# A new layout for the head of a four-layer graph kernel: loads in order of need, weights prepared in six stages

## The chip, the cores and the metric

The kernel runs on one core of a Trainium2 chip. The metric is device time in microseconds (us), the median over several executions; all runs told here were of the same fast state, and the granted TensorE clock over a whole run was 0.98 to 0.99 of full speed in all of them. Only differences of runs that shared a chip are compared as ratios. Times inside a run are counted from the start of its span.

## The reference

```python
h = maximum(layernorm(x), 0); x = x + gated_graph(h)      # layer 0: three sigmoid gates per node,
                                                          #   messages over adj, its transpose, itself
h = maximum(layernorm(x), 0); x = x + attention(h)        # layer 1: causal, adj added to the scores
h = maximum(layernorm(x), 0); x = x + three_convs(h)      # layer 2: (adj*S) @ (h @ W) with W1, W2, W3
h = maximum(layernorm(x), 0); x = x + mlp_batchnorm(h)    # layer 3: normalised adjacency, two linear
                                                          #   maps, batch norm over the whole batch
```

`x` is 128 x 128 x 256, `adj` 128 x 128, all float32. W1 is 256 x 512, W2 512 x 1024, W3 1024 x 256. The batch is worked in 32 groups of 4. Layers 0 to 2 run group by group; layer 3 needs sums over all groups.

## The kernel before

TensorE products are done with seven instead of eight block products, which needs *combinations* (sums and differences of quarters) of both operands. Those of the weights are formed once, in the head, on GpSimd:

```python
def seven_of(b, name):
    b11, b21, b12, b22 = quarters(b)
    extra = weights.tile(...)
    t1, t2, t4n = (extra[:, i] for i in range(3))
    nc.gpsimd.tensor_tensor(t1, b12, b11, ALU.subtract)
    nc.gpsimd.tensor_tensor(t2, b22, t1, ALU.subtract)
    nc.gpsimd.tensor_tensor(t4n, b21, t2, ALU.subtract)
    nc.gpsimd.tensor_tensor(b12, b22, b12, ALU.subtract)
    return b11, b21, b22, t4n, t1, t2, b12
```

The head loads weights from two queues, stages them in a pool that is closed before the "work" pool is opened, and prepares them all before layer 0 of group 0. Then the first two groups alternate:

```python
with tc.tile_pool(name="prep", bufs=1) as prep:
    def turned(dst, src, nr, name):            # transpose on TensorE, copy on VectorE
        ...
        nc.vector.tensor_copy(dst[:, c, :]..., pt)
    ...                                        # adjacency, wqkv, m_qk, w_vo, degrees
    turned(bw1T, bw1, FC, "bw1T")
    turned(bw2t, bw2, DC, "bw2T")
    nc.scalar.dma_start(BW2T, bw2t)
...
w = passA.enter_context(tc.tile_pool(name="work", bufs=2))
...
for _ in layer0(0):
    pass
QR, VR = (seven_of(m, n) for m, n in ((m_qk, "m_qk"), (w_vo, "w_vo")))
W1R = seven_of(w1, "w1")
first, second = layer1(0), layer0(1)
while next(first, first) is not first:
    if next(second, second) is second and not W2R:
        W2R += seven_of(w2, "w2"); W3R += seven_of(w3, "w3"); BW1R += seven_of(bw1T, "bw1T")
```

Layer 0 of a group: the gate products `gs`, then the *gate combinations*, twelve VectorE instructions on two operands in SBUF each (SBUF is the engines' on-chip memory), then products and the addition to x. The profile calls both `cmb` and `bias` by the name of the tile they lie in, `m`:

```python
for b in range(G):                             # G = 4, three gates each: 12 instructions
    nc.vector.scalar_tensor_tensor(gs, h[:, b, :], 1.0, gw[:, i, :], ..., accum_out=gl[...])
...
for b in range(G):
    nc.vector.scalar_tensor_tensor(cmb[:, b, :], aout, gt[:, b, 1:2], cmb[:, b, :], ...)
    nc.vector.scalar_tensor_tensor(cmb[:, b, :], ident, gt[:, b, 2:3], cmb[:, b, :], ...)
for b in range(G):
    nc.vector.scalar_tensor_tensor(bias[:, b, :], oeb, gt[:, b, 1:2], bias[:, b, :], ...)
...
nc.vector.scalar_tensor_tensor(xt, bias, 0.0, xt, ALU.max, ALU.add)     # "x add"
```

## Time and profile before

| | before |
|---|---|
| median of the first 3 runs | 2714.4 us (2713.95 to 2714.87) |
| span of the profiled run | 2709.8 us |
| TensorE busy | 95% |
| first h of group 0 | 29.89 us |
| end of the gate products (gl) | 43.31 us |
| end of the x add of group 0 | 54.86 us |
| first product of layer 2 of group 0 (pu_x) | 99.64 us |
| store of group 0 after layer 2 | 172.79 us |

The last rows are moments on one chain, read from the order of time. Names that begin with p followed by another name (pu_x, pqv, pm, ps, py) are results of TensorE. The differences between neighbours are the stages. The profile's lines for them are in the prediction.

### The profile page before, as it was taken

What the parts mean: (1) busy time and instruction counts of PE and PEld (TensorE: products, weight loads), DVE (VectorE), ACT (ScalarE), POOL (GpSimd) and SP (SyncE); (2) the same over time, 40 slices, a digit from 0 to 9 for tenths busy, and PEclk for the clock granted to TensorE, in tenths of its full rate; (3) what the DMA queues carried; (4) which work ended last, traced back from release to release, by engine and by line L of the source; (5) the groups of instructions that cost most, each with busy time, mean ns of one, the idle gap of its engine ahead of it and who ended that gap; (6) DMA issues with size and microseconds to landing.
All of it is one profiled execution on the core that took longest, in us unless ns stands there. A gap on an engine that the chain in (4) does not pass through costs nothing.

```text
span 2709.8 us, 39136 instructions
## 1 busy us (share of the span) xinstructions
PE 2582.3 (95%) x14831; PEld 2220.0 (82%) x14831; DVE 1899.8 (70%) x4624; ACT 1232.8 (45%) x2435; POOL 469.1 (17%) x484
## 2 busy tenths in 40 slices
PE   3899999999999999999999999999999999979994
PEld 2788888988988988888888898898898888944443
DVE  5677777777777777777777777777877775444445
ACT  2444444445444444544444444544444443334445
POOL 4111111111111111111111111111111111110001
PEclk6899999999999999999999999999999999989997
DMA  3000000000000000000000000000000000034449
GB/s 135 1 17 32 32 32 32 24 32 24 32 32 32 32 32 32 32 23 25 32 32 32 32 24 32 24 32 32 32 32 32 32 24 16 32 148 155 155 169 366
DMA packets 61758, 142.17 MB, mean 52 GB/s; under 512 B 4594, under 2 KB 39940, under 8 KB 57604
## 3 DMA queue, kind: packets, MB, share of 16 engines
q1 hardware_dynamic: 50224, 103.36, 10.6%
q0 software_dynamic: 9216, 33.56, 3.1%
q10 hardware_dynamic: 2132, 2.76, 0.3%
q8 instruction: 117, 1.92, 0.3%
q14 instruction: 69, 0.57, 0.1%
HBM read 73.08 MB, written 66.58 MB: 52 GB/s over the span
## 4 chain that ended last, share of the span: by engine, by line
PE 63%; DVE 21%; ACT 5%; issue 5%; POOL 4%; DMA 2%; ACTq 0%; SPq 0%; DVEq 0%; POOLq 0%
PE p_x L338 10%; PE po L729 8%; PE p_x L321 6%; PE pu_x L321 4%; PE p_z L338 4%; PE pz_x L338 4%; DVE st L258 4%; POOL rs L145 4%; ACT h L267 3%; DVE uT L280 3%; PE p_z L321 2%; PE p_y L338 2%; PE pg L277 2%; PE ps L481 2%; PE pz_z L338 2%
## 5 line engine op out<-in xcount | busy, mean ns | idle before, releaser
L267 ACT ACTIVATE h<-x,sh,rs 128x256 f32<-128x256 f32 x512 | 268.7, 591 | 138.4 <-DVE sh L264 126.2
L145 POOL TENSOR_TENSOR rs<-rs,nhalf 128x4 f32<-128x4 f32 x128 | 130.1, 1016 | 813.4 <-DVE rs L143 813.4
L338 PE MATMUL p_x<-uT,w 128*128 128x256 f32 x1024 | 242.2, 379 | 0.0
L353 ACT COPY p_t<-p_x 128x512 f32<-128x512 f32 (+1 forms) x192 | 98.3, 512 | 301.5 <-PE p_x L338 288.4
L568 ACT ACTIVATE h2T<-h2T 128x512 f32<-128x512 f32 x192 | 120.4, 627 | 233.8 <-DVE h2T L567 233.8
L390 DVE SCALAR_TENSOR_TENSOR gs<-h,gw 128x256 f32<-128x256 f32 x384 | 203.7, 530 | 19.4 <-ACT h L267 6.8
L729 PE MATMUL po<-zi,bw2T 128*128 128x512 f32 x496 | 213.0, 592 | 0.0
L338 PEld LDWEIGHTS p_x<-uT,w 128*128 128x128 f32 x1024 | 189.7, 190 | 23.1
L258 DVE BATCH_NORM_STATS2 st<-x 128x6 f32<-128x256 f32 x512 | 190.7, 414 | 2.9 <-DMA x<-in_x_dram 1.8
L729 PEld LDWEIGHTS po<-zi,bw2T 128*128 128x128 f32 x496 | 94.2, 190 | 118.6 <-issue 107.9
L722 ACT ACTIVATE zi<-zi,sh_bn,sc_bn 128x512 f32<-128x512 f32 x124 | 90.5, 802 | 116.8 <-DMA zi<-z 110.7
L598 POOL DMA_DIRECT2D x<-x x32 | 19.8, 620 | 691.5 <-DVE x L595 691.5
L733 DVE TENSOR_SCALAR o<-po,vecs 128x512 f32<-128x512 f32 x64 | 48.1, 751 | 128.6 <-PE po L729 128.6
L277 PEld LDWEIGHTS pmu<-a2T,u 128*128 128x128 f32 x1024 | 119.8, 192 | 15.0 <-issue 7.4
L321 PEld LDWEIGHTS p_x<-w,h2T 128*128 128x128 f32 x1024 | 124.3, 192 | 3.3
L338 PE MATMUL p_x<-us,w_s 128*128 128x256 f32 x512 | 126.2, 380 | 0.0
L321 PE MATMUL p_x<-w,h2T 128*128 128x128 f32 x1024 | 124.6, 275 | 0.0
L338 PE MATMUL p_x<-uT,w_s 128*128 128x256 f32 x512 | 124.3, 385 | 0.3 <-DVE h2T L567 0.3
L338 PE MATMUL p_y<-uT,w 128*128 128x256 f32 x512 | 121.1, 379 | 0.0
L338 PE MATMUL p_z<-us,w 128*128 128x256 f32 x512 | 121.0, 379 | 0.0
L338 PE MATMUL p_z<-us,w_s 128*128 128x256 f32 x512 | 121.0, 379 | 0.0
L277 PE MATMUL pmu<-a2T,u 128*128 128x128 f32 x1024 | 119.9, 275 | 0.0
(252 smaller groups left out, 6016.1 us busy)
## 6 DMA issues: line engine op xcount, KB each, us to landing
z<-zo SPq DMA_DIRECT2D x62, 512.0 KB, 2.6
zi<-z SPq DMA_DIRECT2D x31, 1024.0 KB, 4.8
x<-in_x_dram SPq DMA_DIRECT2D x32, 512.0 KB, 3.9
x<-x POOLq DMA_DIRECT2D x32, 512.0 KB, 3.0
x3i<-x POOLq DMA_DIRECT2D x32, 512.0 KB, 6.6
out_dram<-x3i SPq DMA_DIRECT2D x64, 256.0 KB, 7.0
w<-in_L_gnn_W_dram SPq DMA_DIRECT2D x1, 2048.0 KB, 11.8
bw<-in_L_gnn_W_dram ACTq DMA_DIRECT2D x2, 512.0 KB
```

Source lines behind the costliest of these rows:

```text
L145: nc.gpsimd.tensor_tensor(dst, src, nhalf[:, : dst.shape[1]], ALU.pow)
L258: nc.vector.bn_stats(st[:, b, :], xt[:, b, :])
L267: nc.scalar.activation(h[:, b, :], xt[:, b, :], AF.Relu, bias=sh[:, b : b + 1], scale=rs[:, b : b + 1])
L277: nc.tensor.matmul(pm[:, b, :], src[:, b, c * P : (c + 1) * P], aT, start=True, stop=True)
L280: nc.vector.tensor_copy(dst[:, c, :], pm.rearrange("p b n -> p (b n)"))
L321: nc.tensor.matmul(pb[:, rr, :], a_r[r][:, c, rr * P : (rr + 1) * P], b_r[r][:, c, :wide], start=(first and rr == 0 and c == 0), stop=(c = ...
L338: nc.tensor.matmul(pb[:, jj, :], b_r[r][:, c, at : at + P], a_r[r][:, c, :], start=(first and jj == 0 and c == 0), stop=(c == nk - 1), ski ...
L353: nc.scalar.copy(t, pb)
L390: nc.vector.scalar_tensor_tensor(gs, h[:, b, :], 1.0, gw[:, i, :], ALU.mult, ALU.mult, accum_out=gl[:, b, i : i + 1],)
L568: nc.scalar.activation(dst, dst, AF.Relu)
L722: nc.scalar.activation(z[j], z[j], AF.Relu, bias=sh1[:, j : j + 1], scale=sc1[:, j : j + 1],)
L729: nc.tensor.matmul(po, bw2T[:, j, i * P : (i + 1) * P], z[j], start=(j == 0), stop=(j == FC - 1),)
```

## The change

The intent is to start the first group sooner and to spread the preparation of the weights over the time in which the engines are idle anyway. Staging tiles move from their own pool into two buffers that layer 2 uses later. The large loads go to SyncE's queue in order of need, which frees ScalarE of issuing them. The copies of the turned weights go from VectorE to ScalarE. The preparation becomes a generator of six stages, and a string says in which order its stages (p), layer 0 and 1 of group 0 (a, B) and layer 0 of group 1 (A) take their steps.

```diff
+    wide1 = w.tile([P, HC2 * T], FP, tag="h2T", name="wide1", bufs=1)
+    wide2 = w.tile([P, 3 * HC2 * T // 4], FP, tag="h2s", name="wide2", bufs=1)
+    wqkv, wT = part_of(wide2, DC, 3 * D), part_of(wide2, 3 * DC, D)
     ... (cut: the other staging tiles likewise)
+    nc.sync.dma_start(wqkv, rows(Wqkv))
+    nc.sync.dma_start(wo, rows(Wo))
+    nc.sync.dma_start(eb, edge_bias)
+    nc.sync.dma_start(oeb, out_edge_bias)
+    load_x(1)
+    nc.sync.dma_start(w1, rows(W1))
+    nc.sync.dma_start(w2, rows(W2))
+    load_x(2)
+    nc.sync.dma_start(w3, rows(W3))
     ... (cut: bw1, bw2 and the vectors)
-                nc.vector.tensor_copy(dst[:, c, :]..., pt)
+            nc.scalar.copy(dst[:, c, :]..., pt)
+    def prepare():
+        turned(wT, wqkv, DC, "wqkvT")
         ... (cut: products m_qk, w_vo)
+        yield
+        SETS["q"], SETS["v"] = seven_of(m_qk, "m_qk"), seven_of(w_vo, "w_vo")
+        yield
+        nc.vector.tensor_tensor(a2T, adjT, adjT, ALU.mult)
+        SETS["1"] = seven_of(w1, "w1")
+        yield
+        SETS["2"] = seven_of(w2, "w2")
+        SETS["3"] = seven_of(w3, "w3")
+        yield
+        turned(bw1T, bw1, FC, "bw1T")
+        turned(bw2t, bw2, DC, "bw2T")
+        nc.sync.dma_start(BW2T, bw2t)
+        yield
         ... (cut: degrees, vectors)
+        yield
+        SETS["b"] = seven_of(bw1T, "bw1T")
-    (cut: the loop that alternates the first two groups)
+    FILL = "apaapaaaaBBABBBBBBBpBABBBApBABBpABBpABBABB"
+    stream = {"a": layer0(0), "p": prepare(), "B": layer1(0), "A": part(layer0, 1)}
+    for k in FILL:
+        next(stream[k])
```

More of the change, by code (lines that the diff above doesn't have):

```diff
@@ L129, with part_of @@
     nc.gpsimd.memset(nhalf, -0.5)
-    nc.scalar.dma_start(eb, edge_bias)
-    nc.scalar.dma_start(oeb, out_edge_bias)
-    for i, w in enumerate((gate_weight, out_gate_weight, loop_gate)):
+    nc.gpsimd.memset(gb, 0.0)
+    for i, v in enumerate((gate_weight, out_gate_weight, loop_gate)):
         nc.scalar.dma_start(
-            gw[:, i, :], bass.AP(tensor=w.tensor, offset=w.offset, ap=[[0, P], [1, D]])
+            gw[:, i, :], bass.AP(tensor=v.tensor, offset=v.offset, ap=[[0, P], [1, D]])
         )
-    nc.gpsimd.memset(gb, 0.0)
     nc.scalar.dma_start(gb[:, 0:1], bias_gate)
     nc.scalar.dma_start(gb[:, 1:2], out_bias_gate)
+    w = passA.enter_context(tc.tile_pool(name="work", bufs=2))
+    small = passA.enter_context(tc.tile_pool(name="small", bufs=4))
+    wide1 = w.tile([P, HC2 * T], FP, tag="h2T", name="wide1", bufs=1)
+    wide2 = w.tile([P, 3 * HC2 * T // 4], FP, tag="h2s", name="wide2", bufs=1)
+    taken = {}
+    def part_of(tile_, *shape):
+        n = 1
+        for k in shape:
+            n *= k
+        at = taken.get(id(tile_), 0)
+        taken[id(tile_)] = at + n
+        flat = tile_[:, at : at + n]
+        return flat.rearrange("p (a b) -> p a b", a=shape[0]) if len(shape) == 2 else flat
+    wqkv, wT = part_of(wide2, DC, 3 * D), part_of(wide2, 3 * DC, D)
+    wo = part_of(wide1, DC, D)
+    bw1, bw2, bw2t = part_of(wide1, FC, D), part_of(wide1, DC, F1), part_of(wide1, FC, D)
+    an, anT, dscr, f = (part_of(wide1, P) for _ in range(4))
+    pos = dscr
+    vrow = small.tile([NV, P], FP, name="vrow", bufs=1)
+    deg = small.tile([P, 4], FP, name="deg", bufs=1)
+    dinv = small.tile([P, 1], FP, name="dinv", bufs=1)
+    nc.sync.dma_start(wqkv, rows(Wqkv))
[7 more added lines that the diff above has]
+    nc.sync.dma_start(w3, rows(W3))
+    nc.sync.dma_start(bw1, rows(bW1))
+    nc.sync.dma_start(bw2, rows(bW2))
+    at = 0
+    for v in (b1, g1, be1, b2, g2, be2):
+        k = v.shape[0] // P
+        nc.sync.dma_start(vrow[at : at + k, :], v.rearrange("(c p) -> c p", p=P))
+        at += k
     def inv_sqrt(dst, src, eps):
@@ L147 @@
     BW2T = scratch.tile([P, FC, D], FP, name="BW2T")
-    with tc.tile_pool(name="prep", bufs=1) as prep:
-        def turned(dst, src, nr, name):
-            ncol = src.shape[-1] // P
-            for c in range(ncol):
-                pt = bank([P, nr, P], f"{name}_{c}")
-                for r in range(nr):
-                    nc.tensor.transpose(pt[:, r, :], src[:, r, c * P : (c + 1) * P], ident)
-                nc.vector.tensor_copy(dst[:, c, :].rearrange("p (r q) -> p r q", r=nr), pt)
-        pa = bank([P, P], "pa")
-        nc.tensor.transpose(pa, adj_sb, ident)
-        nc.vector.tensor_copy(adjT, pa)
-        for dst, src, name in ((ain, adj_sb, "fi"), (aout, adjT, "fo")):
-            pos = prep.tile([P, P], FP, name=f"pos_{name}")
-            nc.vector.tensor_scalar(pos, src, 0.0, None, ALU.is_gt)
-            f = prep.tile([P, P], FP, name=f"origin_{name}")
-            nc.vector.scalar_tensor_tensor(f, src, 0.0, pos, ALU.min, ALU.add)
-            nc.vector.tensor_tensor(dst, f, adj_sb, ALU.mult)
-        wqkv = prep.tile([P, DC, 3 * D], FP, name="wqkv")
-        nc.sync.dma_start(wqkv, rows(Wqkv))
-        wo = prep.tile([P, DC, D], FP, name="wo")
-        nc.sync.dma_start(wo, rows(Wo))
-        nc.sync.dma_start(w1, rows(W1))
-        nc.sync.dma_start(w2, rows(W2))
-        nc.sync.dma_start(w3, rows(W3))
-        bw1 = prep.tile([P, FC, D], FP, name="bw1")
-        nc.scalar.dma_start(bw1, rows(bW1))
-        bw2 = prep.tile([P, DC, F1], FP, name="bw2")
-        nc.scalar.dma_start(bw2, rows(bW2))
-        bw2t = prep.tile([P, FC, D], FP, name="bw2t")
-        vrow = prep.tile([NV, P], FP, name="vrow")
-        at = 0
-        for v in (b1, g1, be1, b2, g2, be2):
-            k = v.shape[0] // P
-            nc.scalar.dma_start(vrow[at : at + k, :], v.rearrange("(c p) -> c p", p=P))
-            at += k
-        nc.gpsimd.affine_select(
-            out=maskb, in_=adj_sb, compare_op=ALU.is_ge, fill=NEG, base=0,
-            pattern=[[-1, P]], channel_multiplier=1,
-        )
-        wT = prep.tile([P, 3 * DC, D], FP, name="wT")
@@ new lines, in turned @@
+    def turned(dst, src, nr, name):
+        ncol = src.shape[-1] // P
+        for c in range(ncol):
+            pt = bank([P, nr, P], f"{name}_{c}")
+            for r in range(nr):
+                nc.tensor.transpose(pt[:, r, :], src[:, r, c * P : (c + 1) * P], ident)
+            nc.scalar.copy(dst[:, c, :].rearrange("p (r q) -> p r q", r=nr), pt)
+    pa = bank([P, P], "pa")
+    nc.tensor.transpose(pa, adj_sb, ident)
+    nc.vector.tensor_copy(adjT, pa)
+    for dst, src in ((ain, adj_sb), (aout, adjT)):
+        nc.vector.tensor_scalar(pos, src, 0.0, None, ALU.is_gt)
+        nc.vector.scalar_tensor_tensor(f, src, 0.0, pos, ALU.min, ALU.add)
+        nc.vector.tensor_tensor(dst, f, adj_sb, ALU.mult)
@@ L198 @@
+    SETS = {}
+    def prepare():
         turned(wT, wqkv, DC, "wqkvT")
@@ L210 @@
                 nc.scalar.copy(dst[:, i, :], pw)
-        nc.vector.tensor_tensor(a2T, adjT, adjT, ALU.mult)
-        an = prep.tile([P, P], FP, name="an")
+        yield
+        nc.gpsimd.affine_select(
+            out=maskb, in_=adj_sb, compare_op=ALU.is_ge, fill=NEG, base=0,
+            pattern=[[-1, P]], channel_multiplier=1,
+        )
+        SETS["q"], SETS["v"] = seven_of(m_qk, "m_qk"), seven_of(w_vo, "w_vo")
+        yield
+        nc.vector.tensor_tensor(a2T, adjT, adjT, ALU.mult)
+        SETS["1"] = seven_of(w1, "w1")
[7 more added lines that the diff above has]
+        yield
         nc.vector.tensor_tensor(an, adj_sb, ident, ALU.add)
-        anT = prep.tile([P, P], FP, name="anT")
         nc.vector.tensor_tensor(anT, adjT, ident, ALU.add)
-        deg = prep.tile([P, 4], FP, name="deg")
-        dscr = prep.tile([P, P], FP, name="dscr")
         nc.vector.tensor_reduce(deg[:, 0:1], anT, AX.X, ALU.add)
@@ L228 @@
         nc.vector.tensor_tensor(deg[:, 3:4], deg[:, 3:4], deg[:, 2:3], ALU.subtract)
-        dinv = prep.tile([P, 1], FP, name="dinv")
         inv_sqrt(dinv, deg[:, 3:4], 0.0)
@@ L234 @@
         nc.vector.tensor_scalar(ahT, ph, dinv, None, ALU.mult)
-        turned(bw1T, bw1, FC, "bw1T")
-        turned(bw2t, bw2, DC, "bw2T")
-        nc.scalar.dma_start(BW2T, bw2t)
         pv = bank([P, NV], "pv")
@@ L247 @@
     X3 = [scratch.tile([P, G, D], FP, name=f"x3_{g}") for g in range(NG)]
-    w = passA.enter_context(tc.tile_pool(name="work", bufs=2))
-    small = passA.enter_context(tc.tile_pool(name="small", bufs=4))
     def norm(g, layer):
@@ L456, in product @@
             nc.tensor.matmul(
-                pb[:, 0, :], QR[r][:, 0, :], hs[r][:, 0, :],
+                pb[:, 0, :], SETS["q"][r][:, 0, :], hs[r][:, 0, :],
                 start=first, stop=True, skip_group_check=True,
@@ L462, in product @@
                     pb[:, 1, rr * P : (rr + 1) * P], hs[r][:, 0, rr * P : (rr + 1) * P],
-                    VR[r][:, 0, :], start=False, stop=True, skip_group_check=True,
+                    SETS["v"][r][:, 0, :], start=False, stop=True, skip_group_check=True,
                 )
@@ L536, in layer1 @@
         yield from seven(
-            rows_by_half(ms, W1R, H1 // 2), put, [P, 2, H1 // 2], f"pu_{g}"
+            rows_by_half(ms, SETS["1"], H1 // 2), put, [P, 2, H1 // 2], f"pu_{g}"
         )
@@ L570, in wide @@
             return seven(
-                columns_by_half(us, W2R, 2 * q), put, [P, 2, T // 2], f"p2_{g}_{q}"
+                columns_by_half(us, SETS["2"], 2 * q), put, [P, 2, T // 2], f"p2_{g}_{q}"
             )
@@ L587, in layer2 @@
             yield next(late)
-        third = seven(rows_by_half(h2s, W3R, P), put_s, [P, 2, P], f"p3_{g}")
+        third = seven(rows_by_half(h2s, SETS["3"], P), put_s, [P, 2, P], f"p3_{g}")
         yield next(third)
@@ L625, in put @@
                     nc.sync.dma_start(Z[g][:, 2 * j : 2 * j + 2, :], z[j])
-        yield from seven(columns_by_half(gs, BW1R, 0), put, [P, 2, T // 2], f"pz_{g}")
+        yield from seven(columns_by_half(gs, SETS["b"], 0), put, [P, 2, T // 2], f"pz_{g}")
     TURN = "CCBCABBCDABCBBCABDDCBADCDDBDCDCBACBBCACACCCbBCBBCBCBBCBCBCBd"
     US = {}
-    W2R, W3R, BW1R = [], [], []
     AHEAD = 3
@@ L638, in part @@
         return f(g) if 0 <= g < NG else iter(())
-    for g in range(1, AHEAD):
-        load_x(g)
-    for _ in layer0(0):
-        pass
-    QR, VR = (seven_of(m, n) for m, n in ((m_qk, "m_qk"), (w_vo, "w_vo")))
-    W1R = seven_of(w1, "w1")
-    first, second = layer1(0), layer0(1)
-    while next(first, first) is not first:
-        if next(second, second) is second and not W2R:
-            W2R += seven_of(w2, "w2")
-            W3R += seven_of(w3, "w3")
-            BW1R += seven_of(bw1T, "bw1T")
-    bs, ds = part(layer1, 1), iter(())
+    FILL = "apaapaaaaBBABBBBBBBpBABBBApBABBpABBpABBABB"
+    stream = {"a": layer0(0), "p": prepare(), "B": layer1(0), "A": part(layer0, 1)}
+    for k in FILL:
+        next(stream[k])
+    assert all(next(stream[k], k) == k for k in "aAB")
+    bs, ds = part(layer1, 1), stream["p"]
     next(bs)
```

## The prediction

> **What bounds the kernel now.** I read the page first, for the busy shares: TensorE is busy 95% of the span, so the long middle can only be shortened by less TensorE work, and the change takes none away. But the first digit of TensorE's row is 3: the head is the exception, and the head is what the change touches.
>
> ```profile
> span 2709.8 us, 39136 instructions
> ...
> PE   3899999999999999999999999999999999979994
> ...
> PEclk6899999999999999999999999999999999989997
> ```
>
> Second, the stretches of 10 us each, which show where TensorE (first column) becomes full.
>
> ```profile
> core 0: us, PE busy (x) PEld busy (x) DVE busy (x) ACT busy (x) POOL busy (x), PEclk, DMA share, GB/s
> ...
> 20.00:30.00 10.00, 3.88 (x18) 3.62 (x18) 3.16 (x8) 0.11 (x1) 9.92 (x11) 0.67 0.87 288
> 30.00:40.00 10.00, 0.00 (x0) 0.00 (x0) 9.13 (x13) 3.25 (x5) 10.00 (x8) 0.50 0.00 0
> 40.00:50.00 10.00, 2.54 (x6) 1.56 (x7) 7.70 (x26) 3.08 (x9) 1.05 (x2) 0.50 0.00 1
> ...
> 90.00:100.00 10.00, 5.15 (x20) 4.33 (x19) 7.07 (x33) 4.15 (x8) 2.85 (x3) 0.67 0.00 1
> 100.00:110.00 10.00, 10.00 (x53) 8.74 (x53) 8.99 (x33) 6.90 (x12) 0.18 (x1) 0.90 0.01 2
> ```
>
> From 100 us on TensorE is full. Before, it is a chain of latencies: load, layer norm, gates, attention of the first group. So **the time is "when does TensorE become full" plus a fixed rest**, and each us by which that moment comes sooner is a us of the whole. I call it the filling point: the first product of the first group's layer 2 (pu_x), at 99.64 us.
>
> Third, the waits and the order of time in the head. ScalarE's first activation (h, the normalised input) has its last operand (sh) at 9.13 us, yet starts at 29.89 us.
>
> ```profile
> ACT h L267 <- DMA BW2T<-bw2t: 11.7, 1, 11.7
> ```
> ```profile
> 8.97 0.16 DVE L264 SCALAR_TENSOR_TENSOR sh<-mv,rs 128x4 f32<-128x4 f32 x1 [1.03 <-POOL rs L145]
> ...
> 15.71 1.28 ACT L210 ACT_TABLE_LOAD   x1 [15.71 <-DMA vrow<-in_L_gnn_g_dram]
> ...
> 24.29 0.37 ACTq L237 DMA_DIRECT2D BW2T<-bw2t  x1
> ...
> 29.89 2.07 ACT L267 ACTIVATE h<-x,sh,rs 128x256 f32<-128x256 f32 x4 [11.69 <-DMA BW2T<-bw2t]
> 30.51 2.35 POOL L294 TENSOR_TENSOR w_s<-w,w_s 128x1024 f32<-128x1024 f32 x1
> 30.52 2.61 DVE L390 SCALAR_TENSOR_TENSOR gs<-h,gw 128x256 f32<-128x256 f32 x1 [6.18 <-ACT h L267]
> ...
> 42.84 0.42 DVE L390 SCALAR_TENSOR_TENSOR gs<-h,gw 128x256 f32<-128x256 f32 x1
> ```
>
> h doesn't read BW2T. But the "work" pool is opened after the "prep" pool is closed and takes its memory, so the first work tile waits for the last reader of prep, which is the store of the turned bw2t, issued at 24.29 and landed some 5.5 us later. That is **20.8 us** (29.89 - 9.13) of a wait for memory, not for data. The last lines show a second loss: the gate products gs take 0.42 us alone (0.46 with their accumulator read) but 1.3 to 2.6 us while GpSimd forms the weight combinations. Also, ScalarE issues loads until 15.7 us, before its first instruction.
>
> **What the Trainium skill says.** "SBUF — State Buffer", section "SBUF: two separate sides": VectorE and GpSimd share a pair of ports as an exclusive lock, held for the whole instruction, taken by VectorE instructions with two SBUF inputs. The trace agrees: 12 gs from 30.52 to 43.28 take 12.8 us against 12 x 0.465 = 5.6 alone, so 7.2 us are lost to some 10.3 us of GpSimd work, about 0.7 us per us. "TensorE: Matmul & The Clock Gate", section "Part 1: The HAM clock gate", says that an idle TensorE runs at half clock; here the granted clock is 0.50 from 30 to 60 us, and the eight matmuls of py take 3.78 us at 87 us and 1.89 us at 140 us. "Trainium Kernel Development and Optimization", section "Key Constraints": queues of different engines run on the same 16 DMA engines, so issuing from several saves issue time only. The trace agrees in that both queues together move about 400 GB/s between 10 and 20 us; so moving loads to one queue makes no bandwidth. It frees ScalarE and sets the order.
>
> **The change, part by part.** The chain from the first h to pu_x, its times from the order of time of before, and what each becomes (all new figures are estimates from these durations):
>
> 1. *Memory.* The staging tiles move into the h2T and h2s buffers, not needed before layer 2 of group 0, after the filling point. h starts when sh is there: **9.2** instead of 29.89 (-20.7). ScalarE has five small issues, over by about 5 us. The input should land as before (5.86). The second of the gate weights landed 8.8 us in; they now go out first.
> 2. *gs.* 12 x 0.465 = 5.6 instead of 12.8 without GpSimd beside it (-7.2): 9.8 to 15.4.
> 3. *Gates to the end of layer 0* (43.31 to 54.86): 11.5 us, unchanged: to 27.0.
> 4. *Norm to first pqv* (54.86 to 63.30 = 8.4): here ScalarE did the four h of group 1 (60.71 to 62.79) ahead of the hT copies, although the transposes were over at 61.1. The new order gives group 0 more steps before those of group 1: 6.8 (-1.6), to 33.8.
> 5. *Seven products and last copy* (63.30 to 74.72 = 11.4): about 1 us was ScalarE work of group 1: 10.4, to 44.2.
> 6. *Scores.* ps started at 79.79, as group 1's eight pm matmuls (76.64 to 80.42, cold clock) stood ahead; the new string has the scores before any gate step of group 1: -5.0.
> 7. *ps to pu_x* (79.79 to 99.64): 19.85, unchanged: to 64.1.
>
> Sum of what is removed: 20.7 + 7.2 + 1.6 + 1.0 + 5.0 = **35.5 us**; the filling point would be 64 us.
>
> What it adds and moves. The turning copies go from VectorE (6 x 0.41 + 2 x 0.69 + 4 x 0.36 = 5.3 us) to ScalarE, which is idle for much of the head: nothing on the path but perhaps 0.5 us around the sigmoid. The **GpSimd combinations don't shrink**: 8 x 0.46 + 4 x 0.73 + 4 x 2.34 + 4 x 1.45 + 4 x 0.72 = 24.6 us. Before, 14 us of them fell in the time in which VectorE waited. Now the chain starts at 9 us, so they fall on it. The order of the program is not the order in which it is run: before, w2 was combined at 22.9 us, ahead of the norm of layer 1 which stands earlier in the text. So I expect a stage to run as soon as its weights have landed, not where the string puts it. Estimated overlap with instructions that have two SBUF inputs: w1 with gs, 2.9 us x 0.7 = 2; m_qk, w_vo and the first of w2 with the gate combinations, 5 x 0.7 = 3.5; x add and small instructions 2.5. Together **+8**. The inverse root of the layer 1 norm (rs) runs on GpSimd too and now queues among instructions of 2.34 us: **+2**. Group 1's layer 0 (about 16 us of VectorE) is later than before and must be done next to the filling stage, where VectorE was already 90% busy (100 to 110 us): **+3** given back.
>
> Net: -35.5 + 8 + 2 + 3 = -22.5 us; with the half us of ScalarE -22. From 2714.4 that is about 2692; as ScalarE and DMA start more freely, I say **2691**.
>
> **Rivals.**
> - *The wait turns into GpSimd's.* If combinations of w2 and w3 stand as a block ahead of rs in GpSimd's queue, or meet the chain fully (24.6 x 0.7 = 17 us), only 10 to 15 us remain: about 2702. For it: GpSimd was 9.9 and 10.0 of 10 busy from 20 to 40 us. Against: loads now come in order of need, so the large ones come late and spread.
> - *Full gain.* Combinations fall into stretches in which VectorE waits for TensorE or ScalarE: -35, about 2679. For it: VectorE was busy only some 60 to 75% of the time from 50 to 100 us.
> - *The head is hidden anyway*: VectorE becomes the bound from 60 to 110 us and TensorE has holes there: -5 to -10, about 2706. Against: VectorE's whole work up to 120 us is about 78 us, less 7 of blocking and 5 moved, 66, which fits between 9 and 84 us, though not easily.
> - *Slower* would need a new wait late in the loop, say for h2T on the store of BW2T. Its data are there by 25 us, its first writer comes after 64 us: hardly.
>
> **Range and chances.** The bound on the gain is 36 to 40 us (1.4%), since the chain itself takes 55 us after 9 us; the 2% threshold (54 us, 2660) would need a shorter middle. A rearranged program also shifts the order of the middle by chance, by an estimated 5 us. So the range is 2677 (full gain and a little) to 2703 (most of it blocked). Faster by over 2%: 0.02; within: 0.97; slower: 0.01.
>
> **What would show it.** Right: the wait of h for BW2T is gone and h starts at 9 to 10 us; gs mean under 0.8 us; pu_x between 64 and 80 us; TensorE full in all 10 us stretches after it; the difference in the filling point equals the difference in time within 5 us; GpSimd's combinations between 12 and 45 us. Wrong in step 1, if h starts much later, on the gate weights, the input or ScalarE's copies; wrong in the overlap, if gs or rs wait long for GpSimd; wrong in the premise (head adds in full), if pu_x comes 30 us sooner and the time falls by less than 15.

## The result, and the profile after

The kernel before took 2714.18 us (median of 4 runs), the changed one **2703.92 us** (2703.71 to 2704.46, 4 runs). The ratio is 0.9963, with an interval of 0.9946 to 0.9981. A ratio here is the mean time of one kernel's fast runs over that of the other's of the same rounds, so it is not quite the ratio of the medians. The gain is 10 us, not 23; the time lies just above the predicted range, which ends at 2703.

Read the chain of the changed kernel first. This is its order of time in the head (start in us, duration in us, engine, line, what it does, and in brackets the idle time before it and its releaser; from 23.83 on only VectorE and GpSimd are shown):

```profile
7.22 1.41 DVE L285 BATCH_NORM_STATS2 st<-x 128x6 f32<-128x256 f32 x4 [2.22 <-DMA x<-in_x_dram]
...
10.34 0.25 DVE L291 SCALAR_TENSOR_TENSOR sh<-mv,rs 128x4 f32<-128x4 f32 x1 [1.03 <-POOL rs L188]
...
10.62 2.08 ACT L294 ACTIVATE h<-x,sh,rs 128x256 f32<-128x256 f32 x4 [2.07 <-DVE sh L291]
...
12.65 0.42 DVE L417 SCALAR_TENSOR_TENSOR gs<-h,gw 128x256 f32<-128x256 f32 x1
...
21.00 0.30 DVE L423 TENSOR_TENSOR gl<-gl,gb 128x12 f32<-128x12 f32 x1
...
23.83 2.52 POOL L319 TENSOR_TENSOR w_s<-w 128x1024 f32<-128x1024 f32 x1
24.07 2.42 DVE L437 SCALAR_TENSOR_TENSOR m<-aout,gt,m 128x128 f32<-128x128 f32 x1
26.42 2.63 DVE L445 SCALAR_TENSOR_TENSOR m<-oeb,gt,m 128x256 f32<-128x256 f32 x1
26.43 2.34 POOL L320 TENSOR_TENSOR w_s<-w,w_s 128x1024 f32<-128x1024 f32 x1
28.73 2.52 POOL L322 TENSOR_TENSOR w<-w 128x1024 f32<-128x1024 f32 x1
28.97 2.42 DVE L440 SCALAR_TENSOR_TENSOR m<-ident,gt,m 128x128 f32<-128x128 f32 x1
```

The wait for memory is gone: h starts 0.28 us after its last operand, at 10.62. But from 23.83 on the new delay is in plain sight, in the *duration* column and not among the waits: each VectorE gate combination ends 0.14 to 0.28 us after one GpSimd combination of w2 or w3. The groups of VectorE instructions by line and shape, within the gates stage (from gl to the end of the x add), put the two kernels side by side (busy us and mean ns of one are the numbers after the bar). Before:

```profile
L418 DVE SCALAR_TENSOR_TENSOR m<-oeb,gt,m 128x256 f32<-128x256 f32 x4 | 1.9, 480 | 0.8 <-ACT m L408 0.8
...
L410 DVE SCALAR_TENSOR_TENSOR m<-aout,gt,m 128x128 f32<-128x128 f32 x4 | 1.3, 344 | 0.0
L413 DVE SCALAR_TENSOR_TENSOR m<-ident,gt,m 128x128 f32<-128x128 f32 x4 | 1.3, 343 | 0.0
```

After:

```profile
L437 DVE SCALAR_TENSOR_TENSOR m<-aout,gt,m 128x128 f32<-128x128 f32 x4 | 6.5, 1650 | 0.1
L440 DVE SCALAR_TENSOR_TENSOR m<-ident,gt,m 128x128 f32<-128x128 f32 x4 | 5.5, 1404 | 0.0
L445 DVE SCALAR_TENSOR_TENSOR m<-oeb,gt,m 128x256 f32<-128x256 f32 x4 | 5.3, 1316 | 0.8 <-ACT m L435 0.8
```

The same twelve instructions take 17.3 us instead of 4.5. The difference, 12.8 us, is the whole growth of the stage (11.55 to 24.43). In the kernel before, GpSimd did three of the four combinations of w2 earlier (22.93 to 30.55), while VectorE waited for memory; the fourth and those of w3 met gs, not the gates.

The second thing to read is the stretch from pu_x, the prediction's filling point, to the store of group 0: one line of the windows for each kernel (length, then busy us and instruction count of PE, PEld, DVE, ACT, POOL). Before:

```profile
99.64:172.79 73.15, 72.71 (x436) 65.42 (x436) 46.32 (x120) 34.43 (x70) 7.55 (x8) 0.98 0.00 1
```

After:

```profile
82.02:163.75 81.73, 77.63 (x466) 68.72 (x466) 57.61 (x145) 38.10 (x79) 12.19 (x13) 0.99 0.02 7
```

TensorE has 4.9 us more work in it (77.63 against 72.71) and 4.1 us of holes (81.73 - 77.63) where there were 0.4. The prediction's yardstick, pu_x, comes 17.6 us sooner, but 8.6 us of that is lost by the store. From there on nothing changes: this is the order of time of GpSimd's queue, the stores of the first and the last group. Before:

```profile
172.79 0.74 POOL L598 DMA_DIRECT2D x<-x  x1 [21.36 <-DVE x L595]
...
2336.09 0.62 POOL L598 DMA_DIRECT2D x<-x  x1 [24.33 <-DVE x L595]
```

After:

```profile
163.75 0.74 POOL L625 DMA_DIRECT2D x<-x  x1 [21.36 <-DVE x L622]
...
2326.99 0.62 POOL L625 DMA_DIRECT2D x<-x  x1 [24.33 <-DVE x L622]
```

The difference is 9.0 us at the first and 9.1 at the last. So the store of group 0 is the right yardstick: **everything that the change does is done in the first 165 us.** (The spans of these two profiled runs differ by 8.2 us, their medians by 10.3; the rest is within the interval.) From here on I count stages up to this store.

### The profile page after: what moved, and what is told of

Its sections match the earlier page's. It is cut to its first block, busy times and chain, and to the rows that moved or that the text cites. A ratio compares the mean times of both kernels' runs of the same rounds, so it can differ in the third digit from the quotient of the medians.

```text
span 2701.6 us, 39124 instructions
## 1 busy us (share of the span) xinstructions
PE 2579.3 (95%) x14831; PEld 2216.3 (82%) x14831; DVE 1877.5 (69%) x4612; ACT 1236.5 (46%) x2447; POOL 477.2 (18%) x484
## 4 chain that ended last, share of the span: by engine, by line
PE 62%; DVE 21%; ACT 6%; issue 5%; POOL 4%; DMA 2%; ACTq 0%; DVEq 0%; POOLq 0%; SPq 0%
PE p_x L365 9%; PE po L750 8%; PE p_x L348 6%; PE pu_x L348 4%; PE p_z L365 4%; PE pz_x L365 4%; POOL rs L188 4%; DVE st L285 4%; ACT h L294 3%; DVE uT L307 3%; PE p_z L348 2%; PE pg L304 2%; PE p_y L365 2%; PE pz_z L365 2%; PE pu_z L348 2%
```

## The experiments

All runs were of 5 rounds; the time before in their rounds was 2712.96 to 2713.68. The stages, in us, read from the order of time of each profiled run:

| run | to h | h to gl | gates | x add to pu_x | pu_x to store | store at | median | ratio |
|---|---|---|---|---|---|---|---|---|
| before | 29.89 | 13.42 | 11.55 | 44.78 | 73.15 | 172.79 | 2714.18 | 1 |
| after | 10.62 | 10.38 | 24.43 | 36.59 | 81.73 | 163.75 | 2703.92 | 0.9963 |
| e1_mem | 17.05 | 19.33 | 14.98 | 45.42 | 73.25 | 170.03 | 2707.07 | 0.9981 |
| e2_nocomb | 11.34 | 10.51 | 12.08 | 36.93 | 81.90 | 152.76 | 2690.09 | 0.9920 |
| e4_dve | 10.92 | 10.54 | 13.11 | 38.98 | 81.60 | 155.15 | 2695.23 | 0.9937 |
| e3_pieces | 10.62 | 10.49 | 15.69 | 39.79 | 81.76 | 158.35 | 2698.72 | 0.9945 |
| e12_memdve | 16.71 | 17.96 | 11.48 | 44.36 | 72.99 | 163.50 | 2703.00 | 0.9961 |
| e7_alt | 10.77 | 10.51 | 24.42 | 44.76 | 72.55 | 163.01 | 2705.26 | 0.9968 |
| e6_upfront | 10.69 | 10.38 | 25.10 | 45.41 | 73.24 | 164.82 | 2703.51 | 0.9966 |
| e5_early | 10.39 | 10.27 | 24.13 | 36.97 | 79.31 | 161.07 | 2701.45 | 0.9960 |
| e8_both | 10.72 | 10.56 | 13.63 | 37.69 | 79.29 | 151.89 | 2693.09 | 0.9925 |
| e9_loads | 9.65 | 9.64 | 14.38 | 38.10 | 79.37 | 151.14 | 2691.64 | 0.9920 |
| e10_lean | 8.82 | 12.26 | 13.64 | 37.56 | 79.26 | 151.54 | 2693.66 | 0.9925 |
| e11_leanalt | 10.32 | 10.75 | 14.33 | 47.57 | 72.87 | 155.84 | 2696.72 | 0.9939 |

The half-widths of the intervals of the experiments' ratios are 0.0012 to 0.0014, some 3.5 us; that of the changed kernel is 0.0018. The changed kernel was not run again in these rounds, so comparisons with it go over different rounds. The stages come from one profile of each kernel: what a run gains at the store differs from what its median gains over the kernel before in its own rounds by up to 3.1 us (e1_mem), so a difference of 2 or 3 us between two runs is a hint and no proof. My theory was that GpSimd's combinations of w2 and w3 took back the gain, in the gates. Its rivals: that the gain was never there (the wait for memory hid something else), that it went in the stretch after pu_x, and that the new order of stages and groups matters by itself.

**Memory alone.** The kernel before, with only the staging tiles moved into the two later buffers; loads, engines and order as before.

```diff
-    with tc.tile_pool(name="prep", bufs=1) as prep:
+    wide1 = w.tile([P, HC2 * T], FP, tag="h2T", name="wide1", bufs=1)
+    wide2 = w.tile([P, 3 * HC2 * T // 4], FP, tag="h2s", name="wide2", bufs=1)
+    (all prep tiles become parts of these)
```

> The kernel before with the staging tiles laid in the h2T and h2s buffers, and nothing else changed (loads, stages, order of the groups as before). Theory (the wait for memory is real, but ScalarE's load issues come next): the first h starts at 16 to 18 us, behind ScalarE's last issue at 15.7, not at 10 and not at 29.9. Theory of the exclusive lock: the twelve gs and the gate combinations then meet GpSimd's combinations of w2 and w3, gates (gl to the end of the x add) 20 us or more instead of 11.5, so that the filling point (pu_x) falls only some 5 to 10 us, to 90 to 95, and the time by the same, since the turned weights stay ahead of it: about 2706 to 2709. Rival (the wait for memory is worth its 13 us): pu_x at 80 to 87, time about 2700.

Measured: 2707.07 us. h starts at 17.05, 12.8 us sooner, held now by ScalarE's own load issues, which end at 15.7 as before, and the table load behind them (in the changed kernel, which has the issues on SyncE, h starts another 6.4 us sooner, at 10.62). But the stages up to the x add grow by 9.3 us together, because gs and the gates now meet what used to run during the wait: the GpSimd combinations, and VectorE's own preparation (its copies of the turned weights alone take 2.7 us between two gs). Two figures of the expectation missed: the gates took 14.98 us, not 20 or more, because with h at 17.05 the combinations of w2 met gs (three of them took 2.37 to 2.44 us) and only the later ones of w3 and bw1T the gates; and pu_x came at 96.78. The store comes 2.8 us sooner, the median is 5.9 us lower. So of the 12.8 us by which the wait was shortened most went to the other engines' work that took its place.

The copies themselves were not held up, though a GpSimd combination ran beside them:

```profile
24.01 2.35 POOL L301 TENSOR_TENSOR w_s<-w 128x1024 f32<-128x1024 f32 x1
24.71 1.40 DVE L184 COPY wide<-bw2T 128x256 f32<-128x256 f32 x4
```

Each of the four took 0.41 us, as the same shape did at 9.65 in the kernel before with no GpSimd work beside it. They read one input, in TensorE's result memory (PSUM); gs and the gate combinations read two in SBUF.

**No combinations of w2 and w3.** The changed kernel without them, so with a wrong result (relative error 2.6).

```diff
-        SETS["2"] = seven_of(w2, "w2")
-        SETS["3"] = seven_of(w3, "w3")
+        for key, m in (("2", w2), ("3", w3)):
+            b11, b21, b12, b22 = quarters(m)
+            SETS[key] = (b11, b21, b22, b21, b11, b22, b12)
```

> The changed kernel without GpSimd's combinations of w2 and w3 (their places hold other quarters: a wrong result on purpose). Theory of the lock: the gates of the first group take about 11.5 us instead of 24.4, pu_x comes 12 to 13 us sooner, at about 69 us. The time: if the give-back after the filling point stays at 5 to 9 us, 2690 to 2694. Rival 1 (gates are slow for another reason, such as ScalarE's copies or the cold TensorE): gates stay above 20 us, time within 2 us of the changed kernel. Rival 2 (what is won before the filling point is lost after it): gates short, pu_x at 69, but the time falls by less than 5 us.

Measured: 2690.09 us. One of the three groups of gate combinations, 1650 ns each in the changed kernel:

```profile
L438 DVE SCALAR_TENSOR_TENSOR m<-aout,gt,m 128x128 f32<-128x128 f32 x4 | 1.3, 355 | 0.1
```

The gates take 12.08 instead of 24.43, the store comes 11.0 us sooner, and the time falls by 13.8 us against the changed kernel's median (from other rounds; by ratios, 0.9920 against 0.9963). These eight instructions, on an engine that is busy 18% of the span, cost about as much as the prediction was short of.

**The same combinations on VectorE.** A correct kernel:

```diff
-    def seven_of(b, name):
+    def seven_of(b, name, engine=nc.gpsimd):
     ...
-        SETS["2"] = seven_of(w2, "w2")
-        SETS["3"] = seven_of(w3, "w3")
+        SETS["2"] = seven_of(w2, "w2", nc.vector)
+        SETS["3"] = seven_of(w3, "w3", nc.vector)
```

> The changed kernel with the combinations of w2 and w3 on VectorE instead of GpSimd (eight instructions, estimated at 1.1 and 0.6 us each, 6.5 us in all; in the order of the program they stand after the gate combinations). Theory of the lock: the gates stage falls from 24.4 to about 14 us (11.5 and two or three combinations that push in), pu_x at 70 to 73, time 2692 to 2697, so faster than the changed kernel although VectorE has more to do. Rival (VectorE is the bound of the head, and the lock a side effect): 6.5 us more work on it make the head longer than in the changed kernel, time 2704 or more.

Measured: 2695.23 us, correct. This is VectorE's order of time in it, at the end of the gates stage:

```profile
27.62 1.21 DVE L319 TENSOR_TENSOR w_s<-w 128x1024 f32<-128x1024 f32 x1
29.88 0.69 DVE L459 TENSOR_TENSOR m<-pm,m 128x512 f32<-128x512 f32 x1 [1.04 <-PE pm L457]
30.48 1.22 DVE L320 TENSOR_TENSOR w_s<-w,w_s 128x1024 f32<-128x1024 f32 x1
31.61 0.68 DVE L459 TENSOR_TENSOR m<-pm,m 128x512 f32<-128x512 f32 x1
```

VectorE does one in 1.21 us where GpSimd took 2.4, and does part of it in the gaps in which it waits for TensorE's pm products (1.0 us of idle time is left of 3.2). The work is not free: the gates take 13.11 and the stage behind them 38.98 us, against 12.08 and 36.93 without any combinations, and the store comes 2.4 us later than there. But giving *more* work to the engine on the critical path gains 8.6 us at the store, since it is no longer locked out. The Trainium skill's "Perfetto Trace Analysis", section "Optimizing Scalar/DVE Operations", says that because the two share a port, "offloading operations between those two might not help". The runs agree and go further: here the offloading to GpSimd cost 8.6 us (163.75 against 155.15 at the store).

**In pieces.** The changed kernel, with the combinations of w2 and w3 still on GpSimd, but cut into pieces of 128 x 256 (24 instructions of some 0.75 us instead of 8 of 1.3 to 2.5).

```diff
-        nc.gpsimd.tensor_tensor(t1, b12, b11, ALU.subtract)
+        for c, e in cuts:                       # 256 elements of a partition at a time
+            nc.gpsimd.tensor_tensor(t1[:, c, e], b12[:, c, e], b11[:, c, e], ALU.subtract)
         ... (the other three likewise, in the same loop)
```

> The changed kernel with GpSimd's combinations of w2 and w3 cut into pieces of 128x256 (24 instructions of about 0.72 us instead of 8 of 2.34 and 1.45). Theory of the lock, one VectorE instruction let in per GpSimd instruction: each of the gate combinations that overlaps waits some 0.7 instead of 2.4 us, so the gates stage falls from 24.4 to 15 to 18 us and pu_x to 73 to 76, time about 2696 to 2699. Rival (the two engines share bandwidth, so that the same total of GpSimd work costs VectorE the same): gates stay at 23 us or more, time 2703 to 2706.

Measured: 2698.72 us; gates 15.69. Its order of time in the gates:

```profile
25.53 0.90 POOL L329 TENSOR_TENSOR w_s<-w,w_s 128x256 f32<-128x256 f32 x1
25.77 0.81 DVE L449 SCALAR_TENSOR_TENSOR m<-ident,gt,m 128x128 f32<-128x128 f32 x1
```

With pieces a gate combination lasts 0.8 to 0.9 us instead of 2.4 to 2.6 beside a whole combination of w2. The rule that these traces show: in a row of GpSimd instructions, VectorE gets in *once per GpSimd instruction*, whatever its length, so each of its instructions that meets one takes as long as that one. In the changed kernel eight of the twelve gate combinations met the eight GpSimd ones (15.0 us in all), so 15.0 less their own 8 x 0.38 = 12.0 us are to be expected; 12.8 were measured. The same reading fits the kernel before: its gs of 1.36 us stood beside combinations of 1.44. The Trainium skill's "SBUF — State Buffer", section "Who interferes with whom", says "Issue order, not op shape, decides who blocks"; the trace agrees, with the addition that in an unbroken row of GpSimd instructions the order is one and one. Not all is won: rs of layer 1 now waits behind the pieces in GpSimd's queue, and the stage after the x add is 3.2 us longer (39.79 against 36.59).

**Two edits to the kernel before.** Memory alone, and w2 and w3 combined on VectorE; nothing of the new order.

```diff
 (the diffs of e1_mem and e4_dve, applied to the kernel before)
```

> The kernel before with two edits only: the staging tiles in the space of h2T and h2s (as in the memory-only run), and w2 and w3 combined on VectorE. The order of its VectorE queue is fixed when it is built: in it the copies of the turned weights (about 4 us) and the eight combinations (some 8 us) stand between the gs instructions of group 0. Theory (work that stands in VectorE's queue between the chain's instructions adds in full, so the new layout's late preparation is worth something once the lock is gone): the gs stage takes 15 to 19 us, the gates stage 11.5 to 13, time 2701 to 2705, so about 4 below the memory-only run. Rival (the lock was all that mattered and the layout is worth nothing): as the changed kernel with the combinations on VectorE, 2694 to 2698.

Measured: 2703.00 us, as much as the whole change. The gates are back at 11.48, but this is VectorE's order of time in the gs stage, which takes 17.96:

```profile
26.68 1.73 DVE L301 TENSOR_TENSOR w_s<-w 128x1024 f32<-128x1024 f32 x1
28.34 0.41 DVE L399 SCALAR_TENSOR_TENSOR gs<-h,gw 128x256 f32<-128x256 f32 x1
28.68 0.08 DVE L399 DVE_READ_ACCUMULATOR gs<-h,gw 128x1 f32 x1
28.68 1.22 DVE L302 TENSOR_TENSOR w_s<-w,w_s 128x1024 f32<-128x1024 f32 x1
```

The combinations stand between the gs, on the path. So the new layout, without the lock, is worth the difference between e12_memdve and e4_dve: 8.4 us at the store (7.8 by the medians). With the lock it is worth 6.3 (3.2 by the medians; e1_mem against the changed kernel). The rival that it is worth nothing falls.

**The order of the two groups.** The changed kernel, with the two groups alternating as before:

```diff
-    FILL = "apaapaaaaBBABBBBBBBpBABBBApBABBpABBpABBABB"
+    FILL = "apaapaaaaBABABApBABABABABpBBpBBpBBBBBBBBBB"
```

> The changed kernel with the two first groups alternating step by step as in the kernel before (stages where they are). Theory (part of the give-back is the later layer 0 of the second group, 2.6 us of TensorE work and 3.7 us of holes after pu_x): pu_x comes some 4 to 8 us later, at 86 to 90, but the stretch from pu_x to the first store of a group falls from 81.7 to 75 to 78 us, so the time is within 3 us of the changed kernel. Rival (the order of the groups is a real gain): time over 2708.

Measured: 2705.26 us. This is the window from its pu_x to its store:

```profile
90.46:163.01 72.55, 72.12 (x436) 64.80 (x436) 46.26 (x120) 34.49 (x70) 7.40 (x7) 0.99 0.00 1
```

pu_x comes 8.4 us later than in the changed kernel, there is no more work and no hole behind it, and the store comes 0.7 us *sooner* (the median is 1.3 us higher; neither is clear of the noise). More came back behind pu_x than expected: 72.55 us, not 75 to 78. The new order of the groups, which the prediction counted as 7.6 us (its steps 4 to 6), had moved TensorE work from before pu_x to behind it.

**All stages first.** The string begins with all six stages, then layer 0, then the alternation:

```diff
-    FILL = "apaapaaaaBBABBBBBBBpBABBBApBABBpABBpABBABB"
+    FILL = "ppppppaaaaaaaBABABABABABABABBBBBBBBBBBBBBB"
```

> The changed kernel with all six stages of weight preparation put in front of the first group's layer 0 in the text (and the first two groups alternating as in the kernel before), loads and memory as in the change. Theory (order of the text matters little for VectorE and GpSimd, which run what has its data; what costs is the GpSimd combinations of w2 and w3 meeting the gates): the gates stage again takes over 20 us, TensorE work is moved as in the alternating run, time 2700 to 2707, as the changed kernel within .2%. Rival (the six stages between the layers are what gains): 2709 or more, with h or gs starting several us later because the preparation stands ahead of it.

Measured: 2703.51 us; h and gl within 0.1 us of the changed kernel. Where the string puts the six stages makes no difference that these runs can see, compared with the changed kernel and with e7_alt (the next runs show a small one where it decides whether TensorE work lies before or behind pu_x). I read this so, without a run that shows it alone: the order of the queues of VectorE and GpSimd is not that of the text, and what the change gains, it gains by memory, queues and engines. The expectation's "run what has its data" is too much: e10_lean below shows an instruction that waits in a fixed order.

**Turned weights early, and both.** e5_early moves the turned weights and the degrees ahead of layer 1 of group 0, because in the changed kernel they ran behind pu_x (TensorE's order of time in the changed kernel):

```profile
84.85 1.04 PE L199 MATMUL bw1T<-ident,wide 128*128 128x128 f32 x8
85.72 1.04 PE L199 MATMUL bw2T<-ident,wide 128*128 128x128 f32 x8
```

e8_both adds to this the combinations on VectorE.

```diff
 (stages 5 and 6 of prepare() moved ahead of stage 3)
-    FILL = "apaapaaaaBBABBBBBBBpBABBBApBABBpABBpABBABB"
+    FILL = "apaapaaaaBppBABBBBBBBpBABBBApBABBABBABBABB"
```

> The changed kernel with the turning of bw1 and bw2, and the degree part, moved ahead of the layer 1 of the first group, so that TensorE does these 18 transposes while it has nothing else to do (in the changed kernel they stand behind pu_x). Theory (give-back = work moved behind the filling point): pu_x at the same time within 2 us, the work of TensorE between pu_x and the first store of a group less by 2.5 us, and the time less by 2 to 3 us: about 2701. Rival (TensorE has holes there anyway and the transposes lie in them): time within 1 us of the changed kernel, 2704.

> e4_dve and e5_early together: combinations of w2 and w3 on VectorE, turned weights early. If the two are independent, the gains add: 8.7 and 2.5 below the changed kernel of their rounds, so about 2692.5 (2690 to 2695), pu_x at 74 to 76. If the earlier turned weights get in the way of the gates when these are short (the transposes wait for bw1 and bw2, which land at about 24 us, and stand in TensorE's queue ahead of the transposes of h), the gain is that of e4_dve alone, 2695 or more.

Measured: 2701.45 and 2693.09 us. In both, the stretch behind pu_x is 2.3 to 2.4 us shorter and the one before it is no longer than that allows (36.97 against 36.59, and 37.69 against 38.98): TensorE has idle time before pu_x for this work. e8_both is 2.1 us below e4_dve, in the medians of different rounds; its pu_x, at 72.60, came sooner than the 74 to 76 expected.

**Gate weights behind x.** e8_both, with the broadcast loads of the gate weights issued on SyncE behind the first x, not on ScalarE ahead of everything.

```diff
-    for i, v in enumerate((gate_weight, ...)):      # on nc.scalar, first of all
+    for i, v in enumerate((gate_weight, ...)):      # on nc.sync, ahead of wqkv
```

> e8_both with the three broadcast loads of the gate weights behind x on SyncE's queue instead of first on ScalarE's. Theory (the broadcasts, issued first, hold x up): the first norm starts at 5.7 to 6.0 us instead of 7.0 to 7.9, as in the kernel before, h at 9.2 to 9.8, pu_x and the time about 1.3 us sooner than e8_both. Rival: the gate weights then land later than h and the first gs waits for them: no gain.

Measured: **2691.64 us** (2691.24 to 2692.94), ratio 0.9920, correct: the lowest median of a correct version, 21.6 us below the kernel before in the same rounds (2713.26). The first norm starts at 6.25 us instead of 7.22 in the changed kernel. That is 1.0 of the 1.4 us by which the changed kernel's h missed the prediction (in the kernel before, the norm started at 5.86). One trace alone would not show this, as the start varies by up to 1.5 us between traces with the same loads; but it lies at 7.00 to 7.94 in the eight traces with these loads first, and at 5.43 to 6.91 in the three with them behind x. Against e8_both of the same rounds the median gains 1.45 us, and the ranges of the two just overlap.

**Two refinements that failed.** e10_lean takes e9_loads, loads w1 last (its combinations met the last gs) and lays the degree matrices into the space of wqkv, to keep their VectorE work behind the first gs.

```diff
-    nc.sync.dma_start(w1, rows(W1))                 # ahead of w2
+    nc.sync.dma_start(w1, rows(W1))                 # behind w3
-    an, anT, dscr, f = (part_of(wide1, P) for _ in range(4))
+    _, _, dscr, f = (part_of(wide1, P) for _ in range(4))
+    an, anT = wqkv[:, 0, :P], wqkv[:, 0, P : 2 * P]
```

> The best version so far (w2, w3 combined on VectorE, turned weights and degrees early, gate weights loaded behind x: 2691.6) with w1 loaded last, so that its GpSimd combinations do not meet gs, and the degree matrices laid in the space of wqkv, so that their first VectorE work cannot stand ahead of the first gs. Theory (time in the chain up to the end of the gates counts in full): gs stage 5.6 to 6.5 us instead of 7.75, first gs within 1 us of h instead of 1.9, first stores 2 to 3 us earlier, time 2688 to 2690. Rival (w1's combinations move from gs into the gates or the norm of layer 1 and cost the same there): gates stage 14 us or more instead of 12.6, time 2691 to 2693.

Measured: 2693.66 us, no better. h starts at 8.82, yet the gs stage grows to 12.26 us. VectorE's order of time shows why:

```profile
12.48 0.29 DVE L244 TENSOR_TENSOR wide<-adj_sb,ident 128x128 f32<-128x128 f32 x1 [3.50 <-PE wqkvT L200]
...
14.03 0.42 DVE L418 SCALAR_TENSOR_TENSOR gs<-h,gw 128x256 f32<-128x256 f32 x1
```

The degree work kept its place in the queue, ahead of gs; it now only waits longer there, for the transposes that read wqkv. A later buffer doesn't change the order of a queue that was fixed when the kernel was built. Both the theory's 5.6 to 6.5 us and the rival's cause (w1 in the gates: they take 13.64, less than e9_loads) were wrong.

e11_leanalt is e10_lean with the alternation of before.

```diff
-    FILL = "apaapaaaaBppBABBBBBBBpBABBBApBABBABBABBABB"
+    FILL = "apaapaaaaBppABABABABABABABpBBpBBBBBBBBBBBB"
```

> As the lean version, but with the first two groups alternating as in the kernel before. Theory (the order of the two groups only moves TensorE work across the first product of layer 2): within .1% of the lean version, the first product of layer 2 some 8 us later, no holes behind it. Rival (with the blocking gone, the new order now shows its gain): 3 us or more slower than the lean version.

Measured: 2696.72 us, 3.1 us slower on the same chip in the same rounds, and no value of its runs overlaps with e10_lean's. My theory of a neutral order falls here: with the turned weights early and the combinations on VectorE, the new order gains 10.0 us before pu_x (47.57 to 37.56) and gives back 6.4 behind it. In the changed kernel it gained 8.2 and gave back 9.2.

## Why the prediction was wrong

It predicted -22.5 us in all, +3 of it behind the filling point, and called the rest fixed. By its steps, against the stages measured up to the store:

| stage | predicted | measured |
|---|---|---|
| to h (step 1) | -20.7 | -19.3 |
| h to gl (step 2, w1's overlap +2) | -5.2 | -3.0 |
| gates (step 3, overlap +3.5) | +3.5 | **+12.9** |
| x add to pu_x (steps 4 to 6, rs +2, small overlap +2.5) | -3.1 | -8.2 |
| pu_x to store (group 1 later, +3) | +3.0 | **+8.6** |
| sum | -22.5 | -9.0 |

- **Step 1 was right** in cause, and 1.4 us off in size: the broadcast loads, issued first, delayed x (e9_loads shows 1.0 of it). That one queue moves about as much as two, the change shows too: 365 GB/s between 10 and 20 us on SyncE's, where the two moved 393 before.
- **Step 2** was right in cause. GpSimd took about what was said; the rest is 2 us of degree work ahead of the first gs and behind it, which the prediction did not count.
- **Step 3 and its overlap are the step that failed**: "m_qk, w_vo and the first of w2 with the gate combinations, 5 x 0.7 = 3.5". The mechanism was right, and the term was mis-sized twice: +3.5 predicted, +12.9 measured. All eight combinations of w2 and w3, 15 us, met the gates, not the first alone; at the prediction's own rate this makes 10.5 us. And the rate is not a constant: under the rule above the loss of a pair is GpSimd's duration less VectorE's own. That gave 0.7 where gs of 0.465 us met GpSimd instructions of 1.35 us on average, and 12.8 of 15.0 us, or 0.85, where combinations of 0.38 met instructions of 1.9. e2_nocomb, e4_dve and e3_pieces show it by removal, by moving, and by size.
- **The gains of steps 4 to 6** came, and more (-8.2; rs did not wait behind GpSimd, so its +2 was 0). But e7_alt shows that in the changed kernel they were displaced, not won (e11_leanalt shows some 3 us of real gain with the other repairs). The +3 for what would be given back was mis-sized: 4.9 us of moved TensorE work and 3.7 us more of holes.
- **The premise** "time is the filling point plus a fixed rest" failed by its yardstick: pu_x is one instruction, and what stands behind it is not fixed when the order changes. The test that the prediction named for this (pu_x 30 us sooner and less than 15 gained) did not trigger, as pu_x moved only 17.6. But another did: pu_x and the time were to move alike within 5 us, and they moved by 17.6 and 10.3.
- The **rival** "the wait turns into GpSimd's" named the right mechanism (combinations of w2 and w3 meeting the chain) and a time, 2702, close to the measured one. That it is so close is in part luck: it did not foresee the -8.2 before pu_x and the +8.6 behind it, which cancel. The observation for it, GpSimd busy 9.9 and 10.0 of 10 us, was in the profile; "loads come in order of need, so the large ones come late and spread" was the argument against it, and w2's combinations ran at 23.83, just as the gates began.
- Two readings of the profile were a little off, without weight for the result: beside GpSimd pieces of 0.90 us, three gs took 0.75 to 0.82 us, not 1.3 or more; and VectorE was busy 48 to 71% of the time from 50 to 100 us, not 60 to 75%.
- Full gain (2679) and a hidden head (2706) are refused: e9_loads shows that some 22 us of the head do reach the end.

What stays open: why the new order of the groups is neutral in the changed kernel and gains 3 us in e10_lean is only read from stages; no run closes the holes behind pu_x (4.1 us against 0.4), which by the view of the waits are two of 1.8 and 1.3 us for ScalarE and shorter ones for VectorE; and no run separates the two halves of e10_lean.

## What to carry to other kernels

When a change starts a latency chain earlier, list what the other engines did during the old wait: it will now run beside the chain. In this kernel it cost one GpSimd duration for each VectorE instruction with two SBUF inputs that met it. A long helper instruction may then be cheaper in the gaps of the engine on the path, or cut into pieces, than "for free" on an idle engine. Measure a gain in the head at a point behind which the order of instructions is the same in both kernels, such as a group's store, and not at the first instruction of a stage.

## What the Trainium skill lacked or had wrong

- "SBUF — State Buffer", sections "SBUF: two separate sides" and "Who interferes with whom": says that the loser blocks for a whole instruction, but not what a row of GpSimd instructions does. Here one VectorE instruction gets in per GpSimd instruction: eight of 0.34 to 0.48 us took as long as eight GpSimd ones (2.42 to 2.63 us each where one stood beside 128 x 1024). Cutting the GpSimd instructions to 128 x 256 made it 0.77 to 0.94.
- "Perfetto Trace Analysis", section "DVE / Act Engine Instruction (TENSOR_ADD, Activation, etc)": gives the profiled start as the start of execution. A lock wait is *inside* the profiled duration: 2.42 us busy with no idle time before it, for 0.34 us of work. So the view of the waits doesn't show it; a mean duration per form does (344 against 1650 ns).
- No page that I read gives a size for it: small broadcast loads issued ahead of a large input delay it, here by about 1 us (first norm at 7.00 to 7.94 in eight traces with them first, 5.43 to 6.91 in three with them behind).
